# Two image layers on one core: correlation channels joined by four, denominators of one more head pair summed on VectorE, and elementwise steps moved to GpSimd

## The chip, the cores and the metric

The kernel runs on one core of a Trainium2 chip, in float32. The metric is the device time of one execution in microseconds. Before the change it is 2643.72 us, the median of three runs (2642.43 to 2647.05).

## What is computed

Eight images of 768 channels and 32 x 32 pixels pass two layers, each behind a group normalisation and added to its input:

```python
x = x + _L0_conv_ref(_gn(x), L0_conv_W_qkv, L0_conv_W_proj, L0_conv_b_proj)
x = x + _L1_conv_ref(_gn(x), L1_conv_conv_w, L1_conv_conv_b)

# layer 0: attention over the 1024 pixels, 12 heads of 64; scores are products of variances
var_v = jnp.var(v, axis=-1, ddof=1, keepdims=True)
var_k = jnp.var(k, axis=-1, ddof=1, keepdims=True)
scores = var_v @ jnp.swapaxes(var_k, -2, -1) * scale
out = softmax(scores) @ v                        # then @ W_proj.T + b_proj

# layer 1: 28 correlations of each pixel's unit vector with shifted ones, and a 1x1 convolution
corr = jnp.stack([jnp.sum(feat_pad[:, :, r:h + r, cc:w + cc] * feat_n, axis=1) for r, cc in _offsets()], axis=1)
out = einsum('bchw,oc->bohw', concatenate([feature, corr], axis=1), conv_w) + conv_b
```

The 28 offsets lie on four lines of seven: 12 distances ahead of the pixel, the same 12 behind it, and the zero distance four times.

## The kernel before

**Order of the work.** Each engine carries out its instructions in the order in which the program issues them. That order comes from a small simulated clock (class `Clock`): a step asks for a later time with `after` or `after_dve` (after VectorE's modelled backlog), sets keys in `ready`, and `work_off` gives TensorE either a group of attention steps or the next unit of the list `rest`. The class `Vector` lets the clock know of VectorE's work; GpSimd's work isn't modelled. All DMAs here but a few at the opening go through SP's queue.

**Stages of an image b.** `KeysValues` computes keys and values in two halves of six heads (28 units each, products saved by a seven-product scheme, banks "x", "y" and "z"; "z" lives in the y pool). `Attention` goes through six pairs of heads; pair 0 to 2 need the first half, 3 to 5 the second. `project` multiplies by the projection. `Corr` forms Gram blocks of the image before (its layer 1), `Conv` does that layer's wide product with correlations. `rest` of image b holds the second half of its keys and values, the Gram blocks and the convolution of image b-1; attention runs between them. In the main loop, while TensorE is busy with one, the other engines prepare the others.

**Attention of a pair.** ScalarE computes exponentials of 128 x 1024 for each of eight key tiles t and two heads (L738), from rows `bc` that a DMA spreads over the partitions. TensorE multiplies them with the values (`products`, L763). The softmax denominators come in one of two ways. Where the pair is listed in `SUMMED`, VectorE adds the exponentials up (`acc`), and four matmuls with ones, into four groups of 32 columns, sum over the partitions (`sum_up`, L797); for the last pair `sum_up_last` does it in two 64-column groups (L847), with reciprocals straight from the bank. Where it isn't, ScalarE computes the exponentials of the transposed scores once more with a running sum (`denominators`, L748), and the inverses go by a transposing matmul (`it`, L340) to DRAM. Inverses come back as `rd` by DMA, and `finish` multiplies the pair's output with them on VectorE. `SUMMED` lists pairs 0, 3, 4, 5 for image 0 and pairs 3, 4, 5 for images 1 to 7.

**The wide products.** `Wide.unit` (for projection and convolution) is six matmuls of 128 x 512 in two halves; each matmul is two records in the trace. `TokenSums` prepares operands t1, t2, third and t4 from the image by three 512-column operations each on VectorE. Units of the products (2, 3, 7, 4) of the convolution also take the correlation channels: `Banks.begin` leaves the bank open, `held` collects two such units, and `join` (L1008) adds one 64-row matmul to each, the second from rows 64 on. A bank is emptied by VectorE after that (`take`), and the next product of the same bank waits for it. In image 7 the correlation goes in apart (`corr`, L1280).

**Correlation channels.** `gather` fills `cs`: 18 channels ahead, the same 18 shifted back and four of the zero distance, 40 in all, of which weights are zero for those that aren't among the 28. A DMA copies them to rows 64 on (`cs<-cs`). Ahead of it, `scale` forms inverse norms `rn` by a power on GpSimd (L1146), VectorE multiplies (`dn`), and `to_dram` transposes on TensorE (`ct`).

**GpSimd** adds up operands of the keys and values (`make_sums`, L600 to L606), copies Gram operands (`turn`, L1086), takes the maximum of the keys over partitions (`most`), and forms inverse deviations.

**Opening.** 36 matmuls of the identity run while image 0 is loaded (L390); then come its group means and deviations and the first units.

Of the kernel before, what the change touches and what calls it, by code (L numbers as in the profile page):

```python
# [13 lines left out]
P = 128  # L14
# [24 lines left out]
NCH = 2 * NA + 4  # L39
# [7 lines left out]
SUMMED = ((0, 3, 4, 5), (3, 4, 5))  # L47
# [7 lines left out]
WARM = 36  # L55
# [13 lines left out]
ORDER = (1, 5, 6, 3, 7, 4, 2)  # L69
OPENING = PAIR[:2] + PAIR[-2:] + PAIR[2:-2]  # L70

# [87 lines left out]
def two_layers(ctx, tc, x, wkv, wproj, bproj, wconv, wcorr, bconv, out):  # L159
# [147 lines left out]
    class TStream:  # L307
        def __init__(self):
            self.keys = []
            for b in range(NB + 1):  # L310
                for kind in ["c"] * (b > 0) + ["p"] * (b < NB):
                    some = PAIR[:-2] if b == NB - 1 and kind == "c" else PAIR
                    self.keys += [(kind, g, p) for g, p in some + SINGLE]
# [28 lines left out]
    class Banks:  # L342
# [11 lines left out]
        def begin(self, g, p, width, pairs, stop=True, between=None):  # L354
            bank = BANK[p]
            of = "x" if bank == "x" else "y"
# [31 lines left out]
    warm = smp.tile([P, 512], F32, tag="sm", name="warm")  # L388
    for n in range(WARM):
        nc.tensor.matmul(warm[:, 0:P], lhsT=ident, rhs=ident, start=True, stop=True)  # L390
# [53 lines left out]
    def load_corr_weights():  # L444
# [5 lines left out]
        for line, step in enumerate(STEP):  # L450
            for j in (1, 2, 3):
                n, k = AHEAD_OF.index(step * j), 3 * line + j - 1
                nc.sync.dma_start(out=wcorr_sb[n : n + 1, :, :], in_=wcorr[k : k + 1, :, :])
                nc.sync.dma_start(out=wcorr_sb[NA + n : NA + n + 1, :, :], in_=wcorr[12 + k : 13 + k, :, :])
        nc.sync.dma_start(out=wcorr_sb[2 * NA : NCH, :, :], in_=wcorr[24:28, :, :])
        nc.sync.dma_start(out=wcorr_sb[HD : HD + NCH, :, :], in_=wcorr_sb[0:NCH, :, :])

# [10 lines left out]
    class Norm:  # L468
# [7 lines left out]
        def means(self):  # L476
            name, mv = self.name, self.mv
            pm = small(f"pm{name}")
            halves(pm[:, 0:1], group_m, mv[:, 0:1])
            self.mean = st.tile([P, 1], F32, tag="mean", bufs=2, name=f"mean{name}")  # L480
# [6 lines left out]
        def spreads(self):  # L487
            name = self.name
            pv = small(f"pv{name}")
            halves(pv[:, 0:1], group_m, self.e)  # L490
            ve = st.tile([P, 1], F32, tag="ve", name=f"ve{name}")
# [216 lines left out]
    class Pair:  # L708
# [131 lines left out]
        def sum_up_last(self):  # L840
# [12 lines left out]
            def invert(n):  # L853
# [3 lines left out]
                if n < 3:  # L857
                    later.after_dve(1.5 if self.b else 0.0, lambda: invert(n + 1))
# [4 lines left out]
            later.after(1.2 if self.b else 0.0, lambda: invert(0))  # L863
# [21 lines left out]
        def finish(self):  # L885
            vector.tensor_tensor(self.ot, self.ot, self.rd, ALU.mult)
            self.finished = True
            self.bk_free = True
            ready.add(("ot", self.b, self.hp))
# [93 lines left out]
    class Wide:  # L983
        def __init__(self, kind, name, acc, bias, operand, finished, more=None):
            self.kind, self.name, self.acc, self.bias = kind, name, acc, bias
            self.operand, self.finished, self.more, self.held = operand, finished, more, []

# [3 lines left out]
        def unit(self, g, p, between=None):  # L991
# [6 lines left out]
            else:  # L998
                self.held.append((*banks.begin(g, p, HF, pairs, stop=False, between=between), taken, *more))
                if len(self.held) == 2:  # L1000
# [3 lines left out]
        def join(self):  # L1004

            for n, (slot, t, taken, i, tokens) in enumerate(self.held):
                at = slice(n * HD, (n + 1) * HD)
# [22 lines left out]
    class TokenSums:  # L1030


        def __init__(self, name, low, high, third=None):
            self.low, self.high = low, high
            self.name = name
            self.third = third or [a[:, HF:] for a in low]
# [4 lines left out]
        def first(self):  # L1041
            self.t1 = self.place(1)
            for k in range(JH):
                a = self.low[k]
                vector.tensor_tensor(self.t1[:, k, :], a[:, HF:], a[:, :HF], ALU.subtract)

        def second(self):
            self.t2 = self.place(2)
            for k in range(JH):
                vector.tensor_tensor(self.t2[:, k, :], self.high[k][:, HF:], self.t1[:, k, :], ALU.subtract)  # L1050

        def thirds(self):
            for k in range(JH):
                vector.tensor_tensor(self.third[k], self.high[k][:, HF:], self.low[k][:, HF:], ALU.subtract)

        def fourth(self):
            self.t4 = self.place(4)
            for k in range(JH):
                vector.tensor_tensor(self.t4[:, k, :], self.high[k][:, :HF], self.t2[:, k, :], ALU.subtract)
# [9 lines left out]
    class Corr:  # L1069
# [70 lines left out]
        def scale(self, hf, dd):  # L1140
# [7 lines left out]
            def columns():  # L1148
# [4 lines left out]
                later.after_dve(0.7, lambda: to_dram(dn))  # L1153
# [19 lines left out]
        def gather(self):  # L1173
# [4 lines left out]
            nc.sync.dma_start(out=u[0:NA, :], in_=r[2:NROW, PAD : PAD + N])  # L1178
            nc.sync.dma_start(out=v[NA:NCH, :], in_=windows(r[0:1, PAD:], (0, NA + 4), (1, N)))
# [356 lines left out]
```

## Time and profile before

| what | value |
|---|---|
| median of three runs | 2643.72 us |
| the profiled execution's own time | 2640.38 us |
| its span, first to last instruction | 2638.7 us |
| granted TensorE clock, mean | 0.998 |
| busy TensorE, VectorE, ScalarE, GpSimd | 2610.0, 1604.3, 1367.3, 413.6 us |
| exponentials for products (L738), 768 | 828.2 us busy, 1138 ns each |
| exponentials with sums (L748), 368 with their read-outs | 420.5 us busy |
| products with values (L763), 3072 records | 700.2 us busy |
| correlation joins (L1008), 168 records | 78.7 us busy, 641 ns each |
| denominators' sums (L797), 136 records | 19.1 us busy, 605 ns each |
| DMA | 446.65 MB, 169 GB/s |

The page of the profile shows one execution: busy time of each engine, the chain of work that ended last, and groups of instructions (line, engine, operation, output and inputs, shape, count, busy time, mean of one, idle time of the engine before them). PE is TensorE, DVE VectorE, ACT ScalarE, POOL GpSimd, SP the engine that issues DMAs. The waits view tells for one engine who ended its idle time (sum, times, longest). The timeline has start, duration, engine, line, operation, and in brackets the idle time before. The ends of matmuls are modelled: a record of 0.59 us overlaps the next, so what a matmul takes from the array is read from start to start.

### The profile page before, as it was taken

How to read it: one execution, taken by the hardware profiler on the slowest of the kernel's cores; microseconds unless marked ns; L12 is line 12 of the kernel's file. 1: busy time of each engine (PE TensorE's matmuls, PEld its weight loads, DVE VectorE, ACT ScalarE, POOL GpSimd, SP SyncE). 2: the span in 40 equal slices, each digit the busy share in tenths (PEclk: the TensorE clock that was granted, in tenths of full speed). 3: DMA queues.
4: the chain of work that ended last, by engine and by line, in shares of the span. 5: the costliest groups of instructions: out<-in, count | busy, mean ns of one | idle time of the engine just before them, and what ended most of it. 6: DMA issues, size and time to landing. Idle time of an engine off the chain costs nothing.

```text
span 2638.7 us, 40466 instructions
## 1 busy us (share of the span) xinstructions
PE 2610.0 (99%) x14766; PEld 1318.2 (50%) x14766; DVE 1604.3 (61%) x4110; ACT 1367.3 (52%) x1841; POOL 413.6 (16%) x444
## 2 busy tenths in 40 slices
PE   9999999999999999999999999999999999999999
PEld 4654566334763347633476334553357433575333
DVE  5858735685447853478534885357853587535864
ACT  1498078711598116980179701897018960199500
POOL 4320130003300033000430003300133001320000
PEclk9999999999999999999999999999999999999999
DMA  7774455455553545626556265562655626545333
GB/s 285 291 247 147 144 198 158 137 182 159 188 187 113 201 153 180 198 95 214 155 172 196 87 220 158 171 205 81 221 172 154 196 84 237 169 137 164 96 117 101
DMA packets 323392, 446.65 MB, mean 169 GB/s; under 512 B 59458, under 2 KB 245170, under 8 KB 323194
## 3 DMA queue, kind: packets, MB, share of 16 engines
q1 hardware_dynamic: 321962, 441.32, 52.0%
q8 instruction: 117, 1.92, 0.3%
q10 hardware_dynamic: 1232, 2.75, 0.3%
q14 instruction: 81, 0.66, 0.1%
HBM read 377.49 MB, written 64.40 MB: 167 GB/s over the span
## 4 chain that ended last, share of the span: by engine, by line
PE 89%; DMA 3%; ACT 3%; DVE 2%; issue 1%; SPq 1%; POOL 1%; DVEq 0%; ACTq 0%; POOLq 0%
PE x L337 35%; PE av L763 22%; PE y L337 17%; PE z L337 9%; PE gr L1101 3%; ACT ex L738 1%; ACT junk L748 1%; DMA x<-x1d 1%; DMA v<-rows 1%; DMA bc<-vdr 1%; PE x L1008 1%; PE den L797 1%; PE y L1008 1%; PE z L1008 1%; DVE acc L153 1%
## 5 line engine op out<-in xcount | busy, mean ns | idle before, releaser
L738 ACT ACTIVATE ex<-bc,nk 128x1024 f32<-128x1024 f32 x768 | 828.2, 1138 | 418.7 <-DMA bc<-vdr 202.6
L763 PE MATMUL av<-ex,v 128*64 128x512 f32 x3072 | 700.2, 596 | 3.4 <-ACT ex L738 3.2
L763 PEld LDWEIGHTS av<-ex,v 128*64 128x64 f32 x3072 | 316.6, 137 | 339.0 <-issue 210.5
L748 ACT ACTIVATE junk<-bk,vm 128x1024 bf16<-128x1024 f32 x368 | 420.5, 1143 | 25.3 <-DMA bk<-kdr 15.5
L153 DVE TENSOR_TENSOR acc<-acc,ex 128x1024 f32<-128x1024 f32 x300 | 344.3, 1209 | 0.0
L215 ACT COPY kp<-x 128x384 f32<-128x384 f32 x28 | 13.4, 477 | 562.1 <-PE x L337 553.4
L337 PE MATMUL y<-kv,s 128*64 128x384 f32 x1488 | 269.4, 487 | 0.0
L337 PE MATMUL x<-kv,xn 128*64 128x384 f32 x1512 | 264.3, 489 | 1.6 <-DVE xn L153 1.6
L337 PE MATMUL x<-kv,s 128*64 128x384 f32 x1488 | 258.2, 486 | 0.0
L337 PEld LDWEIGHTS x<-kv,xn 128*64 128x64 f32 x1512 | 145.3, 138 | 101.1 <-issue 80.5
L337 PEld LDWEIGHTS x<-kv,s 128*64 128x64 f32 x1488 | 145.2, 137 | 91.2 <-issue 67.6
L337 PEld LDWEIGHTS y<-kv,s 128*64 128x64 f32 x1488 | 140.7, 137 | 87.1 <-issue 69.2
L494 POOL TENSOR_TENSOR rstda<-vea,neghalf 128x1 f32<-128x1 f32 x8 | 4.8, 595 | 964.4 <-DVE vea L153 964.4
L1086 POOL TENSOR_TENSOR turn<-f,ones 128x384 f32<-128x384 f32 x112 | 110.9, 1010 | 248.3 <-PE gr L1101 167.6
L337 PE MATMUL z<-kv,xn 128*64 128x384 f32 x768 | 135.1, 486 | 0.0
L337 PE MATMUL x<-v,wt 128*64 128x512 f32 x576 | 131.1, 594 | 0.0
L337 PE MATMUL x<-f,wt 128*64 128x512 f32 x504 | 120.1, 594 | 0.0
L153 DVE TENSOR_TENSOR v<-y,v 128x128 f32<-128x128 f32 x180 | 40.9, 282 | 127.3 <-PE y L337 127.3
L600 POOL TENSOR_TENSOR s<-xn 128x384 f32<-128x384 f32 x64 | 66.8, 1052 | 287.2 <-PE x L337 199.0
L153 DVE BATCH_NORM_STATS2 vbn<-v 128x6 f32<-128x64 f32 x720 | 101.6, 209 | 0.0
L337 PEld LDWEIGHTS z<-kv,xn 128*64 128x64 f32 x768 | 76.4, 137 | 45.9 <-issue 34.3
L1101 PEld LDWEIGHTS gr<-f,turn 128*64 128x64 f32 x1344 | 88.3, 137 | 13.2 <-issue 5.2
(192 smaller groups left out, 3006.5 us busy)
## 6 DMA issues: line engine op xcount, KB each, us to landing
kv<-kvs SPq DMA_DIRECT2D x124, 576.0 KB
kv<-in_wkv_dram SPq DMA_DIRECT2D x95, 576.0 KB
bc<-vdr SPq DMA_DIRECT2D x96, 512.0 KB
f<-in_x_dram SPq DMA_DIRECT2D x48, 512.0 KB
bk<-kdr SPq DMA_DIRECT2D x46, 512.0 KB
x1d<-f SPq DMA_DIRECT2D x42, 512.0 KB
x<-x1d SPq DMA_DIRECT2D x42, 512.0 KB
out_dram<-x SPq DMA_DIRECT2D x82, 256.0 KB
```

The source lines that it names most:

```text
L153: return getattr(self.engine, name)(*args, **kw)
L215: nc.scalar.copy(to, at)
L337: nc.tensor.matmul(out[at], lhsT=lhsT[:, at], rhs=rhs, start=start, stop=stop, **kw)
L494: nc.gpsimd.tensor_tensor(self.rstd, ve, neghalf[:, 0:1], ALU.pow)
L600: nc.gpsimd.tensor_tensor(self.sums[g][:, 0], a[g][2], a[g][3], ALU.add)
L738: nc.scalar.activation(ex, self.bc[e], AF.Exp, scale=self.kv.nk[self.half][:, h, t : t + 1])
L748: nc.scalar.activation(junk, self.bk[e], AF.Exp, scale=self.kv.m2[self.half][:, h, t : t + 1], accum_out=self.sums[:, e, t : t + 1],)
L763: nc.tensor.matmul(self.av[e * HD : (e + 1) * HD, hf, :], lhsT=self.vt[:, t, e, :], rhs=exs[e][:, hf * HF : (hf + 1) * HF], start=t == 0, ...
L797: nc.tensor.matmul(den[at * 32 : (at + 1) * 32, :], lhsT=ones[:, 0:32], rhs=self.acc[e][:, hf * HF : (hf + 1) * HF], start=True, stop=True,)
L1008: nc.tensor.matmul(t, lhsT=wcorr_sb[at, i, :], rhs=cs[at, tokens, :], start=False, stop=True, skip_group_check=True)
L1086: nc.gpsimd.tensor_tensor(to[:, :, side], half, windows(ones, ones.ap[0], (0, J), (HW, 4), (1, HW)), ALU.mult)
L1101: nc.tensor.matmul(ps[side * HD : (side + 1) * HD, :n].rearrange("p (y x) -> p y x", x=WIDE), lhsT=block[:, j, side, :], rhs=image[:, 4 * ...
```

## The change

- Correlation: 28 channels in place of 40 (only those with a weight), stored in four groups of 32 rows; in images 0 to 5 the first eight correlation units are joined by four, in a changed order of products (`QUADS`), of which (0, 2) takes a bank of the small pool; the other four by two. More, smaller gather DMAs, and three copies of `cs` in place of one.
- Pair 0 of images 1 to 7 gets its denominators as VectorE sums.
- On GpSimd: `finish` of every pair but the last of an image, with its key set 2.5 us later in the simulated clock, and the token sums of the convolution for images 0 to 6.
- Order: reciprocals of an image's last pair start at 2.6 in place of 1.2 and are 1.0 in place of 1.5 apart; for image 0 the transposes of the correlation are asked for 3.0 in place of 0.7 after VectorE.
- Opening: 42 identity matmuls in place of 36, and 6 and 12 more beside the first normalisation.

```diff
+PICKED = ((1, 1), (31, 1), (62, 2), (93, 3))
+CHANNELS = [first + apart * n for first, apart in PICKED for n in range(3)]
+NS = len(CHANNELS)
-NCH = 2 * NA + 4
+NCH = 2 * NS + 4
-SUMMED = ((0, 3, 4, 5), (3, 4, 5))
+SUMMED = ((0, 3, 4, 5), (0, 3, 4, 5))
-WARM = 36
+WARM, BRIDGE = 42, (6, 12)
+QUADS = PAIR[:10] + ((0, 2),) + PAIR[10:12] + ((1, 2), (2, 5), (2, 1)) + SINGLE[2:]
+FOUR = P // 4
+def conv_order(b):
+    return QUADS if b < NB - 2 else (PAIR[:-2] if b == NB - 2 else PAIR) + SINGLE
...
         def begin(self, g, p, width, pairs, stop=True, between=None, apart=False):
             bank = BANK[p]
+            if apart:
+                t = other([P, width], f"{bank}{g}")
+                for k, (lhsT, rhs) in enumerate(pairs):
+                    halves(t, lhsT, rhs, start=k == 0, stop=False, skip_group_check=True)
+                return ("apart", g), t
...
-    warm = smp.tile([P, 512], F32, tag="sm", name="warm")
-    for n in range(WARM):
-        nc.tensor.matmul(warm[:, 0:P], lhsT=ident, rhs=ident, start=True, stop=True)
+    warm = avp.tile([P, 512], F32, tag="av", name="warm")
+    def keep_warm(count):
+        for n in range(count):
+            nc.tensor.matmul(warm[:, 0:P], lhsT=ident, rhs=ident, start=True, stop=True)
+    keep_warm(WARM)
...
             halves(pm[:, 0:1], group_m, mv[:, 0:1])
+            if name == "a0":
+                keep_warm(BRIDGE[0])
...
             halves(pv[:, 0:1], group_m, self.e)
+            if name == "a0":
+                keep_warm(BRIDGE[1])
...
-                    later.after_dve(1.5 if self.b else 0.0, lambda: invert(n + 1))
+                    later.after_dve(1.0 if self.b else 0.0, lambda: invert(n + 1))
...
-            later.after(1.2 if self.b else 0.0, lambda: invert(0))
+            later.after(2.6 if self.b else 0.0, lambda: invert(0))
...
         def finish(self):
-            vector.tensor_tensor(self.ot, self.ot, self.rd, ALU.mult)
+            last = self.hp == HP - 1
+            (vector if last else nc.gpsimd).tensor_tensor(self.ot, self.ot, self.rd, ALU.mult)
             self.finished = True
             self.bk_free = True
-            ready.add(("ot", self.b, self.hp))
+            later.after(0.0 if last else 2.5, lambda: ready.add(("ot", self.b, self.hp)))
...
-                self.held.append((*banks.begin(g, p, HF, pairs, stop=False, between=between), taken, *more))
-                if len(self.held) == 2:
+                apart = (g, p) == (0, 2) and self.joined[:1] == [4]
+                self.held.append((*banks.begin(g, p, HF, pairs, stop=False, between=between, apart=apart), taken, *more))
+                if len(self.held) == (self.joined[0] if self.joined else 2):
+                    self.joined = self.joined[1:]
                     self.join()
...
-                at = slice(n * HD, (n + 1) * HD)
+                at = slice(n * FOUR, n * FOUR + NCH)
...
-                vector.tensor_tensor(self.t2[:, k, :], self.high[k][:, HF:], self.t1[:, k, :], ALU.subtract)
+                self.engine.tensor_tensor(self.t2[:, k, :], self.high[k][:, HF:], self.t1[:, k, :], ALU.subtract)
...
-                later.after_dve(0.7, lambda: to_dram(dn))
+                later.after_dve(0.7 if b else 3.0, lambda: to_dram(dn))
...
+            for n, (first, apart) in enumerate(PICKED):
+                k, row = 3 * n, 2 + AHEAD_OF.index(first)
+                nc.sync.dma_start(out=u[k : k + 3, :], in_=windows(r[row : row + 1, PAD:], (apart * ROW, 3), (1, N)))
+                nc.sync.dma_start(out=v[k : k + 3, :], in_=windows(r[0:1, PAD + first :], (apart, 3), (1, N)))
                 nc.sync.dma_start(
-                    out=u[NA + k : NA + k + count, :],
-                    in_=windows(r[2 + k : 3 + k, PAD - first :], (ROW - 1, count), (1, N)),
+                    out=u[NS + k : NS + k + 3, :],
+                    in_=windows(r[row : row + 1, PAD - first :], (apart * (ROW - 1), 3), (1, N)),
                 )
...
-                nc.sync.dma_start(out=cs[HD : HD + NCH, :, :], in_=cs[0:NCH, :, :])
+                for n in range(1, 4):
+                    nc.sync.dma_start(out=cs[n * FOUR : n * FOUR + NCH, :, :], in_=cs[0:NCH, :, :])
...
-            self.sums = TokenSums(f"f{b}", [f[:, k, :] for k in range(JH)], [f[:, JH + k, :] for k in range(JH)])
+            self.sums = TokenSums(f"f{b}", [f[:, k, :] for k in range(JH)], [f[:, JH + k, :] for k in range(JH)], nc.gpsimd if b < NB - 1 else vector)
...
+            self.wide.joined = [4, 4] if self.b < NB - 2 else []
```

## The prediction

> **What bounds the kernel now.** I read the page first: busy time of the engines and the chain that ended last.
>
> ```profile
> PE 2610.0 (99%) x14766; PEld 1318.2 (50%) x14766; DVE 1604.3 (61%) x4110; ACT 1367.3 (52%) x1841; POOL 413.6 (16%) x444
> PE 89%; DMA 3%; ACT 3%; DVE 2%; issue 1%; SPq 1%; POOL 1%; DVEq 0%; ACTq 0%; POOLq 0%
> ```
>
> TensorE is busy 2610.0 of 2638.7 us, so only 28.7 us are open, and a change pays in one of two ways: fewer array passes, or one of the few stalls gone. That VectorE, ScalarE or GpSimd get more or less work is worth nothing by itself. A busy TensorE could still hide pauses under its modelled ends, so I also took the distance from one matmul's start to the next: a unit of the wide layers (12 records) takes 2.58 us, one of the keys and values 1.93 us, throughout. The distances that exceed this by over 0.3 us sum to 27.5 us. The waits of TensorE name most of them:
>
> ```profile
> PE x L337 <- DVE x L153: 4.6, 6, 0.9
> PE ct L340 <- DVE dn L153: 3.3, 1, 3.3
> PE av L763 <- ACT ex L738: 3.2, 2, 2.4
> ```
>
> The first recurs once in each of six images; the others belong to image 1's attention (us 391.8 and 474.7). Two more matter through the clock: the windows view, columns us, PE, PEld, DVE, ACT, POOL, PEclk, DMA share, GB/s, has after the second wait
>
> ```profile
> 391.50:396.30 4.80, 1.47 (x11) 0.45 (x8) 1.08 (x7) 4.77 (x6) 3.23 (x4) 1.00 0.32 102
> 396.30:399.70 3.40, 3.40 (x15) 1.58 (x13) 0.17 (x1) 3.40 (x5) 0.00 (x0) 0.50 0.07 17
> ```
>
> that is, 3.4 us at half clock follow the pause, worth 1.7 us. The same happens at 478.2 (after the third wait) and at 17.4 (after the opening).
>
> **Joins by four.** A join of two today, in TensorE's timeline:
>
> ```profile
> 879.51 2.79 PE L337 MATMUL x<-t4f,wt 128*64 128x512 f32 x12 [0.72 <-DVE x L153]
> 882.24 0.69 PE L1008 MATMUL y<-cs,wcorr_sb 64*128 64x512 f32 x1
> ...
> 882.77 0.59 PE L1008 MATMUL y<-cs,wcorr_sb 64*128 64x512 f32 x1
> ...
> 883.29 1.94 PE L337 MATMUL x<-v,wt 128*64 128x512 f32 x8
> ```
>
> From 882.24 to 883.29 it is 1.05 us: two passes, in each of which both row groups run at once. Four 32-row groups are not in this trace. From above: no overlap between two pairs, 2.10 us, no gain. From below: 1.05 us, all four at once. The nearest row is the denominators' sum, four matmuls in four 32-column groups:
>
> ```profile
> 125.45 1.99 PE L763 MATMUL av<-ex,v 128*64 128x512 f32 x8
> 127.37 1.07 PE L797 MATMUL den<-acc,ones 128*32 128x512 f32 x8
> 128.37 1.08 PE L763 MATMUL av<-ex,v 128*64 128x512 f32 x4
> ```
>
> Eight records take 127.37 to 128.37, 1.00 us. The Trainium skill (TensorE: Matmul & The Clock Gate, Part 3, measured speedup) is less kind: four row tiles of K=32, N=512 gain 3.07 times, not 4. With a lone matmul estimated at 0.86 us (four distances of 0.215 us) that makes 4 x 0.86 / 3.07 = 1.12 us. I take 1.08 us, two pair passes and a little more issue; the rule would take 0.5 us of the total. Images 0 to 5 have 12 such matmuls, now 6 joins, then two of four and two of two: 6 x (6 x 1.05 - 2 x 1.08 - 2 x 1.05) = 6 x 2.04 = **-12.2 us**. Image 6 keeps pairs; image 7 only changes its row offset.
>
> **Pair 0's denominators for images 1 to 7.** Away go 7 x 16 exponentials with a sum on ScalarE, 112 x 1.143 = 128 us, and two 0.11 us transposing matmuls per image. ScalarE is not what ends, so the 128 us count nothing directly, but attention runs some 18 us per image ahead. Added: 14 additions of 1024 columns on VectorE, and one column-group sum on TensorE, which is on the path: 7 x (1.00 - 0.22) = **+5.5 us**. The additions cost, by the page,
>
> ```profile
> L153 DVE TENSOR_TENSOR acc<-acc,ex 128x1024 f32<-128x1024 f32 x300 | 344.3, 1209 | 0.0
> ```
>
> 14 x 1.209 = 16.9 us per image, 118 in all. They run beside the second half's keys and values, whose banks VectorE must empty. Image 0's pair 0 already does exactly this, and no pause over 0.3 us stands between us 18 and 183. I take zero; if that cover failed, one bank late by one addition would be 1.2 us per image, 8 us.
>
> **Moves to GpSimd.** Five of six final products per image (40 x 1.21 = 48 us) and the conv token sums of images 0 to 6 (84 x 0.68 = 57 us) leave VectorE, which thus ends near 1604 + 118 - 105 = 1617 us. On GpSimd the nearest row is
>
> ```profile
> L600 POOL TENSOR_TENSOR s<-xn 128x384 f32<-128x384 f32 x64 | 66.8, 1052 | 287.2 <-PE x L337 199.0
> ```
>
> Scaled by columns: about 2.8 us for 1024 and 1.4 us for 512, together 40 x 2.8 + 84 x 1.4 = 230 us; GpSimd goes from 414 to about 640 us. A rule speaks against it: the Trainium skill (GPSIMD Engine Reference, 4.1 Engine selection, and 1, Specifications) wants elementwise work on VectorE, GpSimd being about twice as slow, and warns that both share an SBUF interface when VectorE reads two SBUF inputs. By the rule up to 230 us of VectorE time could be hit, 1850 us or 70% in the worst case. The trace has four of the 300 additions wholly beside GpSimd work: 1206 ns against 1209 without; GpSimd's own adds go from 1005 to at most 1192 ns. I take the row: no cost to VectorE.
>
> What can cost is order. GpSimd takes its queue in order, and pair 1's product waits for its DMA: VectorE stood 8.2 to 10.7 us before that multiplication in images 2 to 7. The wait now stands on GpSimd, with the token sums, the turned copies, the maximum of the keys and the inverse norms behind it. Of the token sums only the second is close: VectorE finished t2f at 1094.35, and TensorE used it at 1102.56, 8.2 us later. Three GpSimd sums take 4.2 in place of 1.9 us, which leaves 6 us. I take zero, with the bound in the rival below.
>
> **Stalls that go.** The recurrent 0.9 us is VectorE held by a reciprocal and a product:
>
> ```profile
> 875.43 1.76 DVE L153 RECIPROCAL acc<-den 128x256 f32<-128x256 f32 x1 [4.18 <-PE den L847]
> 877.10 1.16 DVE L153 TENSOR_TENSOR v<-v,rd 128x1024 f32<-128x1024 f32 x1
> 878.18 0.68 DVE L153 TENSOR_TENSOR x<-z,x 128x512 f32<-128x512 f32 x1
> 878.77 0.68 DVE L153 TENSOR_TENSOR x<-x,x 128x512 f32<-128x512 f32 x1
> ```
>
> The bank of 878.77 was full at 874.3. The product leaves this queue, and the first reciprocal comes at +2.6 in place of +1.2 us. All six stalls are worth 5.6 us; late next is the last pair's product, which ends no later (+1.4 - 3 x 0.5). I take **-4**. The wait at 391.8 starts on GpSimd:
>
> ```profile
> 391.77 1.96 POOL L1086 TENSOR_TENSOR turn<-f,ones 128x384 f32<-128x384 f32 x2
> 393.71 1.02 POOL L1146 TENSOR_TENSOR rn<-m,neghalf 128x4 f32<-128x4 f32 x1
> ```
>
> and VectorE's dn waits for rn. For image 0 the transposes are now asked for 2.3 us later, so the pause shrinks from 3.5 to 1.2 us and the half clock with it: 2.3 + 1.7 = **-4.0**. The wait at 474.7 comes from ScalarE: after a late DMA it does five sums of pair 2 (6.3 us) before pair 3's exponentials, and a VectorE reciprocal behind the last of them holds the additions. ScalarE being 18 us ahead, those sums fit in its 6 us of idle time before: 2.6 + 1.7 = **-4.3**. The opening: 18 bridging matmuls (0.22 us each) hold TensorE busy, delay the first real one by some 1.5 us and may save the 1.7 us of half clock: **-0.3** (between -1.7 and +1.5). Image 7's correlation waits 0.9 us for a copy of 40 rows, now 28: **-0.5**.
>
> **What is new.** Joining four leaves four banks for VectorE at once, 4 x 0.69 = 2.8 us, and only one unit of 2.58 us before the next needs the second bank (1.4 us when VectorE is free, 3.8 behind two additions). 12 quads at 0 to 1.2 us; I take 0.4, **+5**. Three more gather DMAs and two more copies are about 2 us of SP's queue per image (0.3 us each, the copies up to 0.85); the weights behind them are seven blocks or 18 us ahead, and cs was ready 16 us before its first join: zero.
>
> Sum: -12.2 + 5.5 - 4 - 4.0 - 4.3 - 0.3 - 0.5 + 5 = -14.8 us on the profiled execution (span 2638.7, its time 2640.38, 1.7 around). That execution is 3.3 us under the median of 2643.72; taken off the median it gives **2629 us**. A difference under 0.2%, 5.3 us, is no difference that this kernel's measurement can tell.
>
> **Rivals.** (A, 0.64) As above: 2616 (every stall gone, nothing new: -12.2 + 5.5 - 5.6 - 5.2 - 4.3 - 1.7 - 0.9 = -24.4, and little else to win) to 2638. (B, 0.19) Only the array passes change, since the schedule shifts and other pauses of the same size appear; or the four groups run as two pairs (+12.2) while the stalls go: -6.7 or -2.6, 2637 to 2641. For it: the whole order is rewritten by 18 us. Against: image 0 shows the pattern without pauses. (C, 0.17) Slower: pair 1's product stands on GpSimd directly before the second token sum. Its 10 us wait + 2.8 + 4.2 = 17.0 us stand against the 10.1 us from t2f's start (1092.46) to its use, so TensorE idles 6.9 us in each of six images, 41 us; where the order lets attention fill half, 21 us stay, and with the array's -6.7 it gives +14, 2658. It decides from 1.1 us per image (6.7 / 6). For it: the waits were 8 to 10.7 us. Against: attention is earlier, so that product should mostly be through before the sums.
>
> A gives 2629. A is faster throughout, B in half of its cases and otherwise within the bound, C slower but for 0.03: faster 0.73, same 0.13, slower 0.14. The range 2616 to 2643 leaves out C's greater part.
>
> **What would show it.** Joins of four at 1.0 to 1.1 us from start to start; 12 x "cs" matmuls per image in four groups; VectorE near 1617 and ScalarE near 1245 us busy; GpSimd near 640. Wrong if TensorE waits for t2f, or for GpSimd at all, by over 1 us per image; if quads take 2 us; or if the waits at 392 and 475 remain.

## The result and the profile after

The changed kernel takes **2675.2 us** (median of 4 runs, 2673.3 to 2679.5), against 2643.1 us for the kernel before beside it: ratio **1.0121** [1.0109, 1.0134], slower by 32 us. The profiled execution took 2679.5 us, with a span of 2677.8 us against 2638.7.

The head of the page of the changed kernel, and its chain:

```profile
PE 2625.5 (98%) x14856; PEld 1318.3 (49%) x14856; DVE 1679.7 (63%) x4077; ACT 1242.3 (46%) x1624; POOL 661.2 (25%) x568
PE 85%; DMA 4%; ACT 3%; issue 3%; DVE 2%; POOL 2%; SPq 1%; POOLq 0%; ACTq 0%; DVEq 0%
```

ScalarE is where it was forecast (1245), GpSimd 21 us above (640). VectorE is 63 us above its forecast of 1617. TensorE's share of the chain falls from 89 to 85%: it waits more often. Its waits:

```profile
PE av L786 <- ACT ex L761: 20.7, 14, 2.5
PE ct L349 <- DVE dn L163: 7.9, 6, 1.3
PE x L346 <- DVE f L163: 5.5, 6, 0.9
PE gr L1129 <- POOL turn L1114: 4.7, 10, 1.5
```

Before, attention waited twice for exponentials; now it does so 14 times, and three more kinds of wait recur, in six images or more. Measured by distances from start to start, pauses of TensorE over 0.3 us went from 27 with 27.5 us to 52 with 58.2 us. The span grew by 39 us, and images 2 to 7 by 41: from one image's small variance matmul to the next, each of images 2 to 6 took 323.6 to 324.9 us before and takes 329.4 to 332.4 now (image 7: 315.5 and 323.2). Image 1 gets 2.5 us shorter (280.8 and 278.3).

Image 3 shows four places. **Pair 1** starts late. ScalarE, then TensorE:

```profile
1046.32 0.59 ACT L225 COPY ds<-den 128x512 f32<-128x512 f32 x1 [1.35 <-PE den L820]
1052.44 1.15 ACT L771 ACTIVATE junk<-bk,vm 128x1024 bf16<-128x1024 f32 x1 [5.54 <-DMA bk<-kdr]
...
1053.59 4.25 ACT L761 ACTIVATE ex<-bc,nk 128x1024 f32<-128x1024 f32 x4
```

```profile
1054.78 2.54 PE L786 MATMUL av<-ex,v 128*64 128x512 f32 x7 [1.64 <-ACT ex L761]
```

A sum stands ahead of the exponentials in ScalarE's order, and its row `bk` is not there. Pair 0's accumulators now sit in the two buffers in which these rows are loaded, so the load goes out only after pair 0's denominators. SP's queue:

```profile
1046.93 1.12 SPq L832 DMA_DIRECT2D den<-ds  x4
1048.15 0.82 SPq L750 DMA_DIRECT2D bk<-kdr  x2
```

**The correlation's turn.** Its norms `dn` are scaled on VectorE at the moment when GpSimd does its new work; VectorE and GpSimd side by side:

```profile
1070.15 2.34 DVE L163 COPY dn<-rn 128x4 f32<-128x4 f32 x1 [1.14 <-POOL rn L1174]
1072.40 3.94 DVE L163 SCALAR_TENSOR_TENSOR dn<-dd,rn,mask 128x19 f32<-128x19 f32 x4
```

```profile
1070.09 2.38 POOL L910 TENSOR_TENSOR v<-v,rd 128x1024 f32<-128x1024 f32 x1
1072.41 3.75 POOL L1073 TENSOR_TENSOR t1f<-f 128x512 f32<-128x512 f32 x3
```

A copy of four columns lasts 2.34 us, as long as GpSimd's product (2.38), and the four scalings end with the token sums. Before, such a copy took 0.17 and a scaling 0.23 us. TensorE's `ct` waits 1.3 us for them.

**Pair 3.** Its second accumulator needs the row buffer that pair 2's last sums still read (VectorE's timeline, then TensorE's):

```profile
1126.52 1.30 DVE L163 TENSOR_TENSOR acc<-ex,ex 128x1024 f32<-128x1024 f32 x1
1133.58 1.22 DVE L163 TENSOR_TENSOR acc<-ex,ex 128x1024 f32<-128x1024 f32 x1 [5.76 <-ACT junk L771]
```

```profile
1134.64 2.54 PE L786 MATMUL av<-ex,v 128*64 128x512 f32 x7 [1.12 <-ACT ex L761]
```

In image 4 the same pause is longer and the clock answers (columns as in the windows view of before):

```profile
1463.40:1466.60 3.20, 1.30 (x5) 0.39 (x6) 2.34 (x3) 3.20 (x5) 0.00 (x0) 1.00 0.00 0
1466.60:1470.00 3.40, 3.40 (x10) 0.97 (x8) 3.40 (x4) 3.40 (x4) 0.00 (x0) 0.50 0.02 5
```

**The group norm of the next image** (`x<-DVE f`, 0.9 us, six images). Its small matmul `pva` comes one unit later in TensorE's order than before. VectorE waits 3.33 us for it, and the operation that empties the projection's bank "x" stands behind that wait, so the next product of this bank is held up (VectorE, then TensorE):

```profile
1258.10 0.16 DVE L163 TENSOR_SCALAR vea<-pva 128x1 f32<-128x1 f32 x1 [3.33 <-PE pva L346]
1258.17 0.74 DVE L163 SCALAR_TENSOR_TENSOR f<-x,bproj_sb,f 128x512 f32<-128x512 f32 x1
```

```profile
1258.97 2.80 PE L346 MATMUL x<-t2o,wt 128*64 128x512 f32 x12 [0.92 <-DVE f L163]
```

What was expected of the array is there. A join of four, in TensorE's timeline:

```profile
1152.13 0.69 PE L1035 MATMUL y<-cs,wcorr_sb 28*128 28x512 f32 x1
...
1152.69 0.59 PE L1035 MATMUL y<-cs,wcorr_sb 28*128 28x512 f32 x1
1153.20 1.06 PE L820 MATMUL den<-acc,ones 128*32 128x512 f32 x8
```

From 1152.13 to 1153.20 it is 1.07 us (1.08 forecast), and the joins of image 3 take 2.07 us less than before (2.04 forecast). The denominators' sums of that image cost 0.94 more (0.78 forecast).

### The profile page after: what moved, and what is told of

Read it like the earlier page. It is cut to its first block, busy times and chain, and to the rows that moved or that the text cites. A ratio compares the mean times of both kernels' runs of the same rounds, so it can differ in the third digit from the quotient of the medians.

```text
span 2677.8 us, 40848 instructions
## 1 busy us (share of the span) xinstructions
PE 2625.5 (98%) x14856; PEld 1318.3 (49%) x14856; DVE 1679.7 (63%) x4077; ACT 1242.3 (46%) x1624; POOL 661.2 (25%) x568
## 4 chain that ended last, share of the span: by engine, by line
PE 85%; DMA 4%; ACT 3%; issue 3%; DVE 2%; POOL 2%; SPq 1%; POOLq 0%; ACTq 0%; DVEq 0%
PE x L346 34%; PE av L786 20%; PE y L346 16%; PE z L346 9%; PE gr L1129 3%; ACT ex L761 2%; DMA vdr<-rsv 1%; ACT junk L771 1%; DMA bc<-vdr 1%; POOL turn L1114 1%; DVE dn L163 1%; PE den L820 1%; PE y L1035 1%; PE den L870 1%; PE z L1035 1%
## 5 line engine op out<-in xcount | busy, mean ns | idle before, releaser
L786 PE MATMUL av<-ex,v 128*64 128x512 f32 x3072 | 719.6, 597 | 21.9 <-ACT ex L761 20.7
L786 PEld LDWEIGHTS av<-ex,v 128*64 128x64 f32 x3072 | 323.7, 137 | 363.8 <-issue 213.3
L163 DVE TENSOR_TENSOR acc<-acc,ex 128x1024 f32<-128x1024 f32 x384 | 452.9, 1241 | 0.0
L771 ACT ACTIVATE junk<-bk,vm 128x1024 bf16<-128x1024 f32 x256 | 292.6, 1143 | 47.3 <-DMA bk<-kdr 28.3
L910 POOL TENSOR_TENSOR v<-v,rd 128x1024 f32<-128x1024 f32 x40 | 116.4, 2909 | 532.2 <-DMA rd<-den 326.3
L346 PEld LDWEIGHTS x<-kv,xn 128*64 128x64 f32 x1512 | 133.9, 137 | 111.3 <-issue 93.7
L346 PEld LDWEIGHTS x<-kv,s 128*64 128x64 f32 x1488 | 137.1, 137 | 98.3 <-issue 82.7
L1114 POOL TENSOR_TENSOR turn<-f,ones 128x384 f32<-128x384 f32 x112 | 131.0, 1190 | 195.6 <-PE gr L1129 139.7
L163 DVE TENSOR_TENSOR acc<-ex,ex 128x1024 f32<-128x1024 f32 x64 | 93.8, 1498 | 30.8 <-ACT junk L771 30.2
L1129 PE MATMUL gr<-f,turn 128*64 128x133 f32 (+1 forms) x1344 | 99.6, 276 | 4.7 <-POOL turn L1114 4.7
```

What stands on the lines that cost most here:

```text
L163: return getattr(self.engine, name)(*args, **kw)
L346: nc.tensor.matmul(out[at], lhsT=lhsT[:, at], rhs=rhs, start=start, stop=stop, **kw)
L771: nc.scalar.activation(junk, self.bk[e], AF.Exp, scale=self.kv.m2[self.half][:, h, t : t + 1], accum_out=self.sums[:, e, t : t + 1],)
L786: nc.tensor.matmul(self.av[e * HD : (e + 1) * HD, hf, :], lhsT=self.vt[:, t, e, :], rhs=exs[e][:, hf * HF : (hf + 1) * HF], start=t == 0, ...
L910: (vector if last else nc.gpsimd).tensor_tensor(self.ot, self.ot, self.rd, ALU.mult)
L1114: nc.gpsimd.tensor_tensor(to[:, :, side], half, windows(ones, ones.ap[0], (0, J), (HW, 4), (1, HW)), ALU.mult)
```

## The experiments

The last column is (ratio - 1) x 2643 us. Two such numbers that were not measured side by side are apart by chance by some 5 us.

| run | what | median us | ratio to before | us |
|---|---|---|---|---|
| after | the change | 2675.2 | 1.0121 [1.0109, 1.0134] | +32 |
| e1 | without pair 0's sums | 2625.1 | 0.9933 [0.9913, 0.9953] | -18 |
| e2 | nothing moved to GpSimd | 2647.7 | 1.0027 [1.0019, 1.0035] | +7 |
| e3 | before + joins only | 2635.6 | 0.9975 [0.9964, 0.9986] | -7 |
| e4 | before + pair 0 only | 2663.3 | 1.0080 [1.0066, 1.0094] | +21 |
| e5 | own buffers for pair 0 | 2686.1 | 1.0169 [1.0150, 1.0187] | +45 |
| e5b | e5 and e2 | 2688.9 | 1.0179 [1.0157, 1.0201] | +47 |
| e6 | products on VectorE | 2666.1 | 1.0089 [1.0067, 1.0111] | +24 |
| e7 | e1 and e2 | 2627.2 | 0.9947 [0.9931, 0.9963] | -14 |
| e9 | pair 3's rows due later | 2656.6 | 1.0067 [1.0054, 1.0081] | +18 |
| e10 | e9, pair 1's rows too | 2662.5 | 1.0088 [1.0074, 1.0102] | +23 |
| e11 | e1 and e6 | 2626.5 | 0.9952 [0.9939, 0.9966] | -13 |
| e12 | small matmuls one unit earlier | 2667.2 | 1.0104 [1.0090, 1.0118] | +27 |
| e13 | e10, pair 1's sums held back | 2660.5 | 1.0074 [1.0055, 1.0093] | +20 |
| e14 | e13, e12, later turn | 2685.3 | 1.0168 [1.0147, 1.0189] | +44 |
| e15 | e1 and later turn | 2620.9 | 0.9925 [0.9908, 0.9942] | -20 |
| e16 | e13, head statistics first | 2638.6 | 0.9992 [0.9984, 1.0001] | -2 |
| e17 | e14, head statistics first | 2644.4 | 1.0013 [1.0006, 1.0020] | +3 |
| e18 | e17 and products on VectorE | 2644.9 | 1.0013 [1.0005, 1.0020] | +3 |

The theories, by the letters of the expectations: **P**, pair 0's sums cost by the waits around their buffers and the order; **G**, GpSimd's new work slows VectorE; **J**, the joins cost; later **R**, all that pair 0 costs beyond the array is an order that can be put right. All kernels differ from the changed one unless "before" is named.

### One part at a time: e1 to e4, e7, e11

e1 sets pair 0 back:

```diff
-SUMMED = ((0, 3, 4, 5), (0, 3, 4, 5))
+SUMMED = ((0, 3, 4, 5), (3, 4, 5))
```

> The changed kernel with pair 0 of images 1 to 7 back on ScalarE, all else as changed. Theory P (pair 0's accumulators take both buffers in which pair 1's rows must arrive, so ScalarE stands idle and carries its sums into pair 3's time): the 1.8 us wait in pair 1 and the 1.3 to 2.7 us wait in pair 3 go, with the 0.8 us of array work, about 4.5 us per image: 2675 - 31 = 2644. Theory G (GpSimd's wide operations hold up VectorE): these waits hang on GpSimd and stay; only 0.8 us per image goes: 2669. Theory J (the joins by four cost more than they save): 2669 too.

Measured: -18 us. Pair 0's sums cost 50 us inside the change, more than theory P had given them.

e2 sets the moves back:

```diff
-            (vector if last else nc.gpsimd).tensor_tensor(self.ot, self.ot, self.rd, ALU.mult)
+            vector.tensor_tensor(self.ot, self.ot, self.rd, ALU.mult)
...
-            later.after(0.0 if last else 2.5, lambda: ready.add(("ot", self.b, self.hp)))
+            later.after(0.0, lambda: ready.add(("ot", self.b, self.hp)))
...
-            self.sums = TokenSums(f"f{b}", [f[:, k, :] for k in range(JH)], [f[:, JH + k, :] for k in range(JH)], nc.gpsimd if b < NB - 1 else vector)
+            self.sums = TokenSums(f"f{b}", [f[:, k, :] for k in range(JH)], [f[:, JH + k, :] for k in range(JH)], vector)
```

> The changed kernel with final products and token sums back on VectorE, all else as changed. Theory P: only the 1.5 us wait for dn and some of the 1.1 us of Gram waits go: 2675 - 7 x 2 = 2661. Theory G: nearly the whole loss goes: 2640 or less. Theory J: no change in the joins, 2661 to 2675.

Measured: +7 us, between the theories. The moves cost 25 us here.

e3 is the kernel before with the 28 channels and the joins by four with their changed order of products; all else is as before.

> The kernel before with nothing of the change but the 28 channels and joins by four in the changed order. Theories P and G: the array's 12.2 us are saved, perhaps less some 3 us of waits for banks: 2631 to 2635. Theory J: the four banks at once cost as much as the joins save or more: 2643 or above.

Measured: -7 us, theory J falls. The array gains 12; TensorE's wait for the head statistics, 2.3 us in the kernel before, is 6.7 here and takes some of it back.

e4 is the kernel before with e1's line the other way round.

> The kernel before with nothing of the change but pair 0 of images 1 to 7 on VectorE sums. Theory P: the two waits appear here as well, with 5.5 us of array work: 2643 + 31 = 2674, at least 2660. Theory G: array work alone, 2649. Theory J: 2649.

Measured: +21 us; pair 0 alone costs four times its array work, with nothing on GpSimd. Its image 3 pauses 2.4 us at the start of pair 1 and 1.1 us at the group norm, but not in pair 3.

e7 is e1 and e2 together.

> The changed kernel without pair 0's sums and without the moves to GpSimd: joins, order and opening remain. If the moves to GpSimd gain by themselves, this is slower than the 2625 with them: 2630 to 2635, near the 2636 of the joins alone less about 4 us for the later transposes of image 0. If they cost something by themselves too, it is below 2625.

Measured: -14 us. So pair 0 costs 21 us (e2 - e7) when nothing is moved and 50 (after - e1) when it is; and the moves are worth -4 us without pair 0 (e1 - e7, within chance), +25 with it. Together they cost 46 us (after - e7), about twice what they cost one at a time.

e11 leaves pair 0 and the products out and keeps the token sums on GpSimd.

> The changed kernel with pair 0 and the final products back, only the token sums on GpSimd. It tells whether the 2.3 us wait for dn that the kernel with pair 0 back still has comes from the products beside it: if so, some 5 us below its 2625, 2620; if the token sums do it, 2625; if the moves gain nothing at all, 2627 as with all back.

Measured: -13 us, 1 us from e7: the sums on GpSimd neither gain nor cost there. The wait for `dn` is as large as in e1 (7.9 us in all), so it does not come from the products.

### Port or wait: e6

e6 takes only the first two changes of e2.

> The changed kernel with only the final products back on VectorE; token sums stay on GpSimd. Theory G: the copy into dn no longer stands beside a GpSimd product, but its multiplications still beside the token sums: half of the 27 us that both together cost, 2662. If the products' wait for their DMA on GpSimd's queue is what counts, nearly all of it: 2650. If the token sums' port use is what counts: 2672.

Measured: +24 us, 8 below the change, between the 2662 of theory G and the 2672 of the token sums' use of the port. The wait of `ct` is gone from the trace; those of attention and of the group norm stay.

### Buffers: e5 and e5b

Pair 0's accumulators get buffers of their own, and pair 1's rows may load at once:

```diff
+                    apart = self.b and not self.hp
+                    places = ((rdpool, "rd"), (uvpool, "uv")) if apart else ((bkpool, "bk"),) * 2
...
-                    if not hp or (before.bk_free if before.summed else before.passes["s"] >= MT * (e + 1)):
+                    if not hp or (self.b and hp == 1) or (before.bk_free if before.summed else before.passes["s"] >= MT * (e + 1)):
```

> The changed kernel, but pair 0 of images 1 to 7 adds up in two tiles that are free at that time (those of the inverses and of the gather), and pair 1's rows for the denominators are asked for at once. Theory P (the two row buffers are the cause): the wait of 1.8 us in pair 1 goes in all seven images, and that in pair 3 at least in part, since ScalarE isn't late any more: 2675 - 7 x 2.1 = 2660 or less, with no idle time of ScalarE for bk in pair 1. Theory G (only GpSimd's port use counts): ScalarE's idle time goes but not the waits: 2670 or more.

> As the kernel with own buffers, with final products and token sums on VectorE too. Theory P: from the 2648 of the kernel with these back, 7 x 1.4 to 2.1 us less: 2634 to 2638. Theory G: no further gain, 2648.

Measured: +45 and +47 us. Theory P failed in both, in its simple form that the shared buffers are the cost. Theory G's bound for e5 (2670 or more) was met, but e5b, with nothing moved to GpSimd, is as slow, where G had 2648. Waits of TensorE in e5, then in e5b:

```profile
PE x L346 <- POOL t2f L1080: 28.0, 12, 7.4
PE av L786 <- ACT ex L761: 9.8, 8, 3.8
```

```profile
PE av L786 <- ACT ex L761: 31.5, 13, 4.7
```

Attention does start earlier (pair 1's wait is 0.95 us in both), but other things come at the wrong time. In e5b pair 3 waits 3.1 to 4.7 us in each of images 2 to 7: VectorE stands before a final product whose inverses are late, and pair 3's additions, for which ScalarE waits, stand behind it (VectorE, then ScalarE):

```profile
1135.08 1.23 DVE L163 TENSOR_TENSOR v<-v,rd 128x1024 f32<-128x1024 f32 x1 [10.42 <-DMA rd<-di]
1136.22 2.36 DVE L163 TENSOR_TENSOR acc<-ex,ex 128x1024 f32<-128x1024 f32 x2
```

```profile
1137.53 8.42 ACT L761 ACTIVATE ex<-bc,nk 128x1024 f32<-128x1024 f32 x8 [6.34 <-DVE acc L163]
```

In e5 TensorE waits for the token sum `t2f`; GpSimd's timeline in its image 3:

```profile
1124.14 0.56 POOL L700 PARTITION_ALL_REDUCE most<-top  x1 [8.31 <-PE x L346]
1134.65 3.71 POOL L1080 TENSOR_TENSOR t2f<-f,t1f 128x512 f32<-128x512 f32 x3 [9.95 <-issue]
```

The all-reduce for the keys' maximum is short, but GpSimd starts nothing for 9.95 us after it, and the profile names no one it waits for. TensorE's pause before `t2f` is 4.3 us here.

### Order: e9, e10, e12, e13

The kernel's order is written from estimates of when things are ready. e9 tells it that pair 3's rows come 6 us later; e10 adds the same for pair 1's:

```diff
+            if kind == "c" and self.hp == HP // 2 and self.b:
+                self.rows_at[kind, e] += 6.0
+            if kind == "k" and self.hp == 1 and self.b:
+                self.rows_at[kind, e] += 3.0
```

> The changed kernel; only the order is made with pair 3's rows expected 6 us later (images 1 to 7), so that ScalarE takes pair 2's remaining sums before pair 3's exponentials. Theory R (the order written out ahead counts on DMAs that are some 5 us faster than they are, and the change moves the places where this shows): the 1.3 to 2.7 us wait in pair 3 goes, with the half clock after it in three images: 7 x 1.9 + 5 = 18 us less, 2657. Theory G (port use alone): no change, 2675.

> As the kernel before it, with pair 1's rows for the denominators expected 3 us later as well. Theory R: the 1.8 us wait in pair 1 goes too, since ScalarE goes on with exponentials: 7 x 1.8 less again, 2645. Theory P (pair 0's hold on the row buffers delays ScalarE whatever the order): no further gain, 2657.

Measured: e9 +18 us, 14 below the change and as R had it; the half clock is gone (granted clock 1.000). e10 +23 us: ScalarE's order in pair 1 did not change, so this run can't tell the two theories apart.

e12 asks for a group norm's two matmuls one unit earlier:

```diff
-                later.after_dve(3.0, norm.spreads)
+                later.after_dve(1.0 if b > 1 else 3.0, norm.spreads)
```

> The changed kernel; only the two small matmuls for the next image's deviations stand one unit earlier in TensorE's order, in six images. If the 1.1 us wait at that place comes from the order alone, 6.6 us less: 2669. If VectorE's load is the cause, 2675.

Measured: +27 us, some 5 below the change, though the intervals touch. In its trace this wait is gone from all six images.

e13 also keeps pair 1's sums behind exponentials until their row is nearly due:

```diff
+                def may():
+                    at = pair.rows_at.get(("k", e))
+                    return None if at and self.b and pair.hp == 1 and at > clock.now + 1.0 else at
```

> As the kernel with pair 3's and pair 1's rows expected later, and ScalarE's order takes a sum of pair 1 only when its rows are expected within 1 us, not ahead of exponentials because none is allowed at that moment. In that order the exponentials of two more key tiles now stand before pair 1's first sum. Theory R (the order is the cause): the wait of 1.4 to 1.9 us in pair 1 goes in seven images, from the 2657 of pair 3's rows alone to 2645. Theory P (the row buffers that pair 0 holds): pair 1 waits as before or the wait moves to its last sums, 2657 or more.

Measured: +20 us, no gain over e9; theory P had the number, but the wait in pair 1 is gone, as R had it. Its trace has none of the recurring waits for `ex`, `dn` and `f` left. A new one has come, 14.5 us in all: TensorE's transposing matmul `ptv` for the second half's head statistics, in e13's image 3 (the timelines of TensorE, VectorE and SP's queue):

```profile
1111.17 0.31 PE L349 MATMUL ptv<-ident,vm 128*48 128x128 f32 x1 [3.00 <-DVE vm L163]
```

```profile
1108.73 0.75 DVE L163 SCALAR_TENSOR_TENSOR x<-x,bconv_sb,x 128x512 f32<-128x512 f32 x1 [6.78 <-DMA x<-x1d]
...
1110.87 0.24 DVE L163 SCALAR_TENSOR_TENSOR vm<-hdv,hsv 128x48 f32<-128x48 f32 x1
```

```profile
1101.52 1.13 SPq L863 DMA_DIRECT2D rd<-di  x2
1102.74 0.54 SPq L1246 DMA_DIRECT2D x<-x1d  x1
```

The statistics stand on VectorE behind the convolution's first residual addition, whose tile `x1d` is reloaded when the keys and values are done, here behind pair 1's inverse rows.

### All orders at once: e14, e16, e17, e18

e14 is e13 with e12's line and `later.after_dve(3.0, lambda: to_dram(dn))` in all images.

> As the kernel before it, with the small matmuls of the deviations one unit earlier and the correlation's transposes 3.0 in place of 0.7 after VectorE in all images. Pair 0's sums and all moves to GpSimd are kept; the order alone differs from the changed kernel. Theory R: all recurring waits are gone, 2675 - 18 - 12 - 8 - 7 = 2630, with the 5.5 us of array work of pair 0 left against the 2625 without it. If VectorE's and GpSimd's work itself limits, 2645 or more.

Measured: +44 us, a miss. The same wait for `vm` is up to 6.3 us an image there, 29.5 in all.

e16 and e17 are e13 and e14 with the statistics ahead of that addition:

```diff
-                later.after(KV_US + 0.5, lambda: later.after_dve(0.0, lambda: self.spread(half)))
+                later.after(KV_US + 0.2, lambda: self.spread(half)) if half and self.b > 1 else later.after(KV_US + 0.5, lambda: later.after_dve(0.0, lambda: self.spread(half)))
```

> The kernel with pair 1's sums held and the rows of pair 1 and 3 later (2660.5 us), and one more change of order: in images 2 to 7 VectorE takes the second half's head statistics (ten operations of 0.2 us) ahead of the convolution's first residual addition, not behind it. In that kernel this addition waited 6.8 us for its reloaded tile, and TensorE's transposing matmul for the statistics waited 3.0 to 3.2 us in each of six images. Theory R (what pair 0 cost beside its array work is order, and each wait can be placed away): the wait goes, 19 us, and the half clock that follows it, some 5 us more: 2637. Theory D (the reloaded tile is late for everything, since its buffer is free only when the keys and values are done): the wait moves to the bank of that addition, 2652 or more. The line is drawn at 2645.

> The kernel with all changes of order (2685.3 us), where the same wait was 6.3 us in each of six images and made up most of TensorE's pauses, with the same statistics taken first. Theory R: 38 us for the wait and some 8 for half clock go: 2640, and below e16 if the earlier small matmuls and transposes are worth anything still. Theory D: the wait moves to the bank, 2665 or more.

> The same as the one with all orders and the statistics first, with the five final products per image on VectorE instead of GpSimd, as before the change. Theory G (sharing between VectorE and GpSimd costs time wherever pair 0 is summed): 5 us or more below e17. Theory R: within 4 us of it, since no order is left in which anyone waits for the slowed operations.

Measured: e16 **-2 us** (2638.6; R had 2637), e17 +3 (2644.4; R had 2640, D 2665 or more). VectorE in e16:

```profile
1101.38 0.25 DVE L163 SCALAR_TENSOR_TENSOR vm<-hdv,hsv 128x48 f32<-128x48 f32 x1
1107.70 0.75 DVE L163 SCALAR_TENSOR_TENSOR x<-x,bconv_sb,x 128x512 f32<-128x512 f32 x1 [6.08 <-DMA x<-x1d]
```

The wait for `x1d` is still 6.1 us, but nobody is behind it who is due. The waits of TensorE in e16:

```profile
PE x L346 <- POOL t2f L1084: 5.5, 1, 5.5
PE gr L1135 <- POOL turn L1120: 4.4, 9, 1.5
```

Images 2 to 6 take 323.1 us each, within 0.04 us of one another, with one pause over 0.25 us left in image 3. All of pair 0's sums and all of GpSimd's work are still in this kernel: 34 us came back by order alone. e18 is 0.4 us from e17, so the products on GpSimd cost nothing in this order; the token sums were not tried there. In e17 the small matmuls of e12 wait 0.7 us an image for VectorE: in the new order they are too early.

### The better version: e15

e15 is e1's line with the turn asked for later in all images, since e1 waited there (`ct`) in four images, up to 2.2 us.

> The changed kernel with pair 0 back on ScalarE and the correlation's transposes 3.0 after VectorE in all images: the fastest kernel so far (2625) without its waits for dn, 7.9 us with 1.7 us of half clock after two of them: 2615. If the wait only moves, 2625.

Measured: **2620.9 us**, ratio 0.9925 [0.9908, 0.9942], faster than both kernels and midway between the two numbers expected. It is 2 us from e1, which is within chance; in the trace TensorE's wait for `dn` is down from 7.9 to 1.3 us. Its images 2 to 6 take 321.2 us with no pause over 0.25 us in image 3.

## Why the prediction was wrong

**Right: the array work.** Joins of four (1.07 us, -2.07 an image), denominators (+0.94), and that the waits at 392 and 475 would shrink or go in the change (0.6 of the 3.5 us at 392 is left; the half clock, though, now follows Gram pauses at 367). The six waits of 0.9 us behind the reciprocals are gone, and the 5 us for banks after joins of four did not come. Without pair 0 the working comes to -14.8 - 5.5 + 4.3 = -16 us, since the gain at 475 rests on ScalarE's lead (e15 still waits 2.7 us there); e1 measured -18, e15 -20, and most of the difference is the 5 us that did not come. On joins the rule of speedup (1.12) was further off than the row of pairs.

**The step that failed: "Image 0's pair 0 already does exactly this ... I take zero", with 8 us if the cover failed.** Pair 0's sums cost 21 us beside the old engines (e4; e2 - e7) and 50 inside the change, of which 5.5 are the array's. The additions are covered in the sense that the step meant: VectorE's banks are not late. But image 0's attention runs beside keys and values alone; from image 1 on the correlation's Gram blocks and norms, the convolution and its reloads lie there too. The hold on the row buffers stood in the precedent as well. In the kernel before, ScalarE waits in image 0 for pair 1's row, but TensorE has 17.65 us of keys and values ahead of its next attention step (ScalarE, then TensorE):

```profile
134.10 1.15 ACT L748 ACTIVATE junk<-bk,vm 128x1024 bf16<-128x1024 f32 x1 [3.65 <-DMA den<-ds]
```

```profile
131.85 2.11 PE L337 MATMUL x<-kv,s 128*64 128x384 f32 x12
...
149.50 4.89 PE L763 MATMUL av<-ex,v 128*64 128x512 f32 x22
```

That there was no pause showed the cover, not that nothing was late. The precedent had the instructions, not the neighbours.

**With it "ScalarE ... counts nothing directly, but attention runs some 18 us per image ahead".** The 18 us were counted as room. With attention taking its turns earlier, the keys and values end later: in image 3 155 us after its start, against 141 before and in e15. So the reloads, pair 1's inverses and the convolution's start fall together, and each queue written by estimated times then had something in front that was not there: sums before their rows (pair 1), sums before pair 3's additions, the group norm's matmuls a unit late. Rival B named this ("the whole order is rewritten by 18 us") with pauses of the old size; they were twice as much. e9 and e12 took two of these waits away by placing alone; e16 took back 34 us. Some 8 of these are not pair 0's: the wait for `dn` (7.9 us) is in e1 too and gone from e16. Against e15, where it is gone as well, pair 0's sums still cost 18 us (e16 - e15), of which 5.5 were the forecast for the array. Most of the rest lies in image 1 (284.0 us, against 275.1 in e15), with its one wait of 5.5 us for `t2f`.

**"I take the row: no cost to VectorE."** The four additions of that row are not typical. In the lines view of VectorE, changed kernel:

```profile
L163 DVE TENSOR_TENSOR acc<-acc,ex 128x1024 f32<-128x1024 f32 x384 | 452.9, 1241 | 0.0
L163 DVE TENSOR_TENSOR acc<-ex,ex 128x1024 f32<-128x1024 f32 x64 | 93.8, 1498 | 30.8 <-ACT junk L771 30.2 <-ACT ex L761 0.6
...
L163 DVE SCALAR_TENSOR_TENSOR dn<-dd,rn,mask 128x19 f32<-128x19 f32 x64 | 31.6, 553 | 1.3 <-DMA dd<-windowed 1.3
```

The last has a mean of 232 ns before. The kernel before had rows that showed this, too: `m<-dd` of four columns takes 154 ns alone (9 times) and 819 ns on average beside GpSimd's turned copies (7 times). VectorE, then GpSimd:

```profile
1032.72 0.95 DVE L153 TENSOR_SCALAR m<-dd 128x4 f32<-128x4 f32 x1 [0.88 <-DMA dd<-windowed]
```

```profile
1031.65 1.99 POOL L1086 TENSOR_TENSOR turn<-f,ones 128x384 f32<-128x384 f32 x2 [5.18 <-PE gr L1101]
```

Taken over all of the trace's instructions, those that lie beside GpSimd exceed their lone time by 75 us in all (14 before), about the 63 us above the forecast. The Trainium skill (GPSIMD Engine Reference, 1. Specifications) was right that the two share an interface when VectorE reads two SBUF operands, as both `acc` rows do; the copy into `dn`, with one operand, was held up as well (2.34 us). The upper bound by the rule, 230 us, was three times too high. How much reaches the end hangs on the order: the moves cost 25 us in the changed kernel (after - e2), 8 of them by the products (after - e6), nothing without pair 0 (e1 - e7), and the products nothing in e18.

**Rival C** gave the right sign for a wrong reason. TensorE does not wait for `t2f` in the change. Where it does (28 us in e5, 5.5 in e16), the product is through, and what stands in front is the pause after the all-reduce, which the prediction's working had not priced.

**What stays open.** Within pair 1 the share of the buffers and that of the order were not told apart: e5 and e10 moved other things too. Nor were the moves' 25 us divided between slower VectorE operations and the waits in GpSimd's queue. I did not take apart the pauses below 0.3 us that follow each wait, nor why e10 lies above e9.

## What to carry to other kernels

When a step takes work off an engine that is not the bound and its consumer runs earlier for it, list what will now lie side by side, queue by queue, and which buffers the next stage needs; a precedent elsewhere in the kernel counts only with the same neighbours. In an order written from estimated times, waits do not add: taking one away can bring a larger one (e14), so look at the trace after each, find what stands in front of the late instruction, and place that. Try an edit's parts alone and together: here two that cost nothing and 21 us alone cost 46 together.

## What the runs showed of the hardware

- A small VectorE operation with SBUF operands can last as long as the GpSimd instruction beside it: the scaling of 128x19 took 231 ns alone and 1264 ns on average beside GpSimd (20 of them, all with four fifths of their time or more beside it), a copy of four columns 2.34 us. By the same count first additions of 1024 columns went from 1216 to 1790 ns (11), later ones from 1210 to 1368 (33). The convolution's residual addition, which reads PSUM, did not change (744 and 751 ns).
- GpSimd loses as well: its product of 1024 columns took 2375 ns without VectorE at work (8 of them) and 3043 ns on average otherwise (32); its turned copies 1010 ns alone (8) and 1558 ns with four fifths of their time or more beside VectorE (37).
- After an all-reduce GpSimd's next ordinary instruction, where one was due, came 7 to 11 us later, often with no wait shown ("issue": 7.7 to 8.2 in the kernel before, 9.95 in e5, 10.39 in e16). In every trace a pair of `MODIFY_POOL_CONFIG` instructions of GpSimd's sequencer stands right behind the all-reduce (1124.66 and 1124.70 in e5), and another pair stands ahead of it. The Trainium skill (GPSIMD Engine Reference, 2.1 Instruction dispatch) gives about 6 us for the first call of freshly loaded code, with no instruction in the profile; the runs agree in kind and show more. Whether it is code loading was not tried. A token sum moved to GpSimd moves behind this.
- TensorE's clock was halved for about 3.4 us after pauses of 2.06 and 2.68 us in pair 3 and 1.90 in pair 1, but not after others of 1.98 and 2.35 us: the length of the pause alone does not decide. The stretches at half clock last 3.413 us and begin whole multiples of that apart (321, 97 and 171 in the change; 111 and 24 before). When pauses are added up within such 3.413 us stretches, the four that half clock followed held 1.9 to 2.5 us of pause; the pause of 2.35 us lay across two, with 1.3 and 1.0 us. One with 1.96 us was not followed by half clock, so this does not give a sharp limit.
